# Layer 1's windowed self-attention: scores for one half's 64 keys, scores placed between projections, values last from two copies

## The chip, the cores and the metric

The kernel runs on one core of one Trainium2 chip. A time is the device time of one execution in microseconds (us). Three runs of the kernel before took 2820.73, 2821.43 and 2823.51 us; their median is 2821.43 us. The profile is of one further execution. Engines are named as in the profile: PE (TensorE matmul), PEld (TensorE weight load, which overlaps PE), DVE (VectorE), ACT (ScalarE), POOL (GpSimd) and SP (SyncE, which here issues most DMAs).

## The reference

A two-layer perceiver block works on 256 tokens of width 512 and a context of 25088 tokens, all in f32. Each layer has cross-attention, self-attention and a mixture of experts, each added to the tokens. The change concerns the self-attention of the second layer ("layer 1"), which works on windows of 128 tokens after a shift by 64:

```python
if SHIFTED:
    x = jnp.roll(x, -DISP, axis=1)              # DISP = 64, b, s, d = 1, 256, 512
xw = x.reshape(-1, w, d)                        # w = 128: two windows
qkv = xw @ w_qkv + b_qkv                        # then q, k, v of 16 heads, 32 wide
attn = jnp.einsum('nhqd,nhkd->nhqk', q, k) / jnp.sqrt(jnp.float32(d_k))
if SHIFTED:
    mask = _create_mask(w)                      # 0 between the first 64 and the last 64
    attn = jnp.where(mask == 0, jnp.float32(NEG), attn)
attn = jax.nn.softmax(attn, axis=-1)
vals = jnp.einsum('nhqk,nhkd->nhqd', attn, v)
out = vals.transpose(0, 2, 1, 3).reshape(n, w, d) @ w_o + b_o
if SHIFTED:
    out = jnp.roll(out.reshape(b, s, d), DISP, axis=1)
```

The mask sets a score to -9e15 wherever query and key lie in different halves of a window. So a token attends to the 64 keys of its own half alone, and in both windows half of the 128 x 128 scores of each head become zero weights.

## The kernel before

The 256 tokens `x` stay in SBUF as two tiles of 128 (T = 2). A normalised and transposed copy `xT` (`norm_T`, which for this layer also applies the shift while it copies) has features on the partitions, 4 blocks of 128 (DC = 4). The program is one long sequence. Most of its time goes to the context of the second cross-attention; then come the stage that is changed, a routing over 8 experts, and the experts' matmuls, whose weights are fetched by SP once the routing has produced expert numbers. The order on each engine is left to a scheduler, except that matmuls written as `queue << ...` stay in the order of the program on PE.

[...]Six form a ring (`ring`, `take`, `give`), from which `ps_mm` hands out the oldest one in turn; two more (`ps_ac`) are separate. A tile that is written into a bank has to wait until the bank's previous content has been read.

The stage in question is `self_attention`, which layer 0 uses as well. It is called from L1044 with the mask `halves` (a constant made by three POOL memsets at L146 to L148), one key block for each of the two token tiles, and `roll=64`. Its steps:

1. `norm_T` (L171): normalise, transpose on PE (L184), copy out (L187, L189).
2. `feature_major` (L198): queries for all heads, then keys, 16 matmuls each of 128x256 (L203), evicted by DVE with their bias (L209).
3. Values: for each token tile 4 matmuls of 128x512 (L239), evicted by DVE (L243).
4. `attention_blocks` (L249): for each token tile t and each group `qp` of eight heads, `weights` and then `attend` of the group before. `weights` makes eight score matmuls (L259) of 32 rows (the width of a head) by 128 keys, four heads side by side in the array's rows, and then, for each pair of heads r, adds the mask on DVE (L270), takes the maximum (L273), and exponentiates on ACT with the sum as a by-product (L275). A reciprocal (L280) and four multiplies (L282) normalise. `attend` transposes the weights on PE (L294), copies them out on any engine (L295), and multiplies with the values (L301): 128 keys deep, 32 columns wide, four heads side by side in the array's columns. DVE copies the result to `oT` while it undoes the shift (L311, L313).
5. `project_out` (L213): for each token tile four matmuls of 128x512 (L217) and two additions (L195, L196).

Weights for the stage are fetched earlier, at the end of the cross-attention, into freed buffers. The rows of biases for it come by a POOL DMA just ahead of it (L1035, L100).

Of the kernel before, what the change touches and what calls it, by code (L numbers as in the profile page):

```python
# [9 lines left out]
F32 = mybir.dt.float32  # L10
AF = mybir.ActivationFunctionType
ALU = mybir.AluOpType
AX = mybir.AxisListType
PSUM = bass.MemoryType.PSUM

P = 128
D = 512
NT = 256
T = NT // P
DC = D // P  # L20
H = 16
HD = D // H
# [5 lines left out]
SCALE = 1.0 / math.sqrt(HD)  # L28
# [9 lines left out]
def perceiver_kernel(  # L38
# [7 lines left out]
    nc = tc.nc  # L46
# [24 lines left out]
    def ps_mm(shape=None):  # L71
        tile, home = take("mm", shape)
        give(home)
        return tile
# [21 lines left out]
    rows = {}  # L96
# [45 lines left out]
        pattern=[[-1, 2 * P]], channel_multiplier=1,  # L142
    )

    halves = const.tile([P, P], F32, name="halves")
    nc.gpsimd.memset(halves, 0.0)  # L146
    nc.gpsimd.memset(halves[0:64, 64:128], -9e15)
    nc.gpsimd.memset(halves[64:128, 0:64], -9e15)  # L148


    class InOrder:

# [67 lines left out]
                )  # L220
            add_rows(t, ps, row)

    def self_attention(xT, wo, col_q, row_v, row_o, blocks, load_qkv, roll=0, fill=None):

        fill = fill or (lambda n: None)
        with tc.tile_pool(name="sa", bufs=1) as sa:
            v = sa.tile([P, T, D], F32, name="v_sa")
            oT = sa.tile([P, DC, NT], F32, name="oT")
            qT = sa.tile([P, DC, NT], F32, name="qT_sa")
            kT = sa.tile([P, DC, NT], F32, name="kT_sa")  # L230
            with tc.tile_pool(name="saw", bufs=1) as saw:
                wqkv = load_qkv(saw)
                xT = xT()
                feature_major(qT, wqkv[0], xT, col_q)
                feature_major(kT, wqkv[1], xT, col_q + 1)
                for t in range(T):
                    ps = ps_mm()
                    for dc in range(DC):
                        queue << nc.tensor.matmul(  # L239
                            ps, xT[:, dc, t * P : (t + 1) * P], wqkv[2][:, dc, :],  # L240
                            start=dc == 0, stop=dc == DC - 1,
                        )
                    nc.vector.tensor_add(v[:, t, :], ps, rows[row_v])  # L243
            with tc.tile_pool(name="sas", bufs=2) as sas:
                attention_blocks(sas, qT, kT, v, oT, blocks, roll, fill)
            fill(1)
            project_out(oT, wo, row_o)

    def attention_blocks(sas, qT, kT, v, oT, blocks, roll, fill):  # L249
        def weights(t, qp):  # L250

            keys, mask = blocks[t]
# [34 lines left out]
        def attend(t, qp, e):  # L287
            keys, _ = blocks[t]
            pT = sas.tile([P, 4, 2, 2, P], F32, tag="pT", name="pT", bufs=1)
            for r in range(4):  # L290
                tp = ps_ac([P, 2, 2, P])
                for i in range(2):
                    for kb in range(len(keys)):
                        queue << nc.tensor.transpose(tp[:, i, kb, :], e[:, r, i, kb * P : (kb + 1) * P], ident)  # L294
                nc.any.tensor_copy(pT[:, r, :, : len(keys), :], tp[:, :, : len(keys), :])  # L295
            av = ps_mm([P, 2, P])
            for i in range(2):
                for kb, kt in enumerate(keys):
                    for r in range(4):
                        h = 4 * (2 * qp + i) + r  # L300
                        queue << nc.tensor.matmul(  # L301
                            av[32 * r : 32 * r + 32, i, :],
                            v[:, kt, h * HD : (h + 1) * HD],
                            pT[:, r, i, kb, :],
                            start=kb == 0 and i == 0, stop=kb == len(keys) - 1,
                            skip_group_check=True,
                        )
            at = (t * P + roll) % NT
            first = min(P, NT - at)
            q2 = slice(2 * qp, 2 * qp + 2)  # L310
            nc.vector.tensor_copy(oT[:, q2, at : at + first], av[:, :, :first])  # L311
            if first < P:
                nc.vector.tensor_copy(oT[:, q2, : P - first], av[:, :, first:])  # L313

        pending = None
        for t in range(T):
# [5 lines left out]
                pending = (t, qp, e)  # L322
        fill(1)
        attend(*pending)

    def rank_of(pool, vals, shape):

# [485 lines left out]
    with tc.tile_pool(name="xa", bufs=2) as xa:  # L813
# [121 lines left out]
        def attend(first, last, qp, es, v):  # L935
            for i in range(2):
                for r in range(4):
                    h = 4 * (2 * qp + i) + r
                    queue << nc.tensor.matmul(  # L939
                        acc[qp][32 * r : 32 * r + 32, i, :],  # L940
                        v[:, h * HD : (h + 1) * HD], es[qp][:, 4 * i + r, :],
                        start=first and i == 0, stop=last, skip_group_check=True,
                    )
# [97 lines left out]
    nc.vector.scalar_tensor_tensor(slot, iota, float(P), ps, ALU.mult, ALU.add)  # L1041
    ffn_scope = ExitStack()
    ffn = ffn_scope.enter_context(tc.tile_pool(name="ffn", bufs=2))
    self_attention(  # L1044
        lambda: norm_T(roll=64), l1a_wo, C_L1A_BQ, R_L1A_BV, R_L1A_BO,
        [([0], halves), ([1], halves)], lambda pool: l1a_wqkv, roll=64,
    )
    ctp_scope.close()

    experts = ExitStack()  # L1050
# [292 lines left out]
```

## Time and profile before

| | |
|---|---|
| median of three runs | 2821.43 us |
| the profiled execution's own time | 2821.5 us |
| its span, first to last instruction | 2819.7 us |
| start of the stage's first projection matmul (L203) | 2465.83 us |
| last score-and-value matmul ended, output projection (L217) starts | 2518.05 us |
| last output projection result reaches DVE (L195) | 2526.56 us |
| granted TensorE clock, mean over the span | 0.985 |
| granted clock from 2488.6 to 2518 us | 0.70 |

Times inside the span are counted from its first instruction. A row of the time line has the start, the length, the engine, the source line and operation, what is written and read, the shape, the count, and in brackets how long the engine had been idle and what ended that. A row of the stretches has the busy time of each engine, with the number of instructions in brackets, then the granted clock (1.00 is full speed), the share of the DMA engines in use and GB/s. A row of the waits says who waited for whom: total, how often, longest.

In f32 a matmul leaves two records on PE and two on PEld; a transpose leaves one. "32*128" behind a matmul is the size of the stationary part: rows of the array by columns.

### The profile page before, as it was taken

What the parts mean: (1) busy time and instruction counts of PE and PEld (TensorE: products, weight loads), DVE (VectorE), ACT (ScalarE), POOL (GpSimd) and SP (SyncE); (2) the same over time, 40 slices, a digit from 0 to 9 for tenths busy, and PEclk for the clock granted to TensorE, in tenths of its full rate; (3) what the DMA queues carried; (4) which work ended last, traced back from release to release, by engine and by line L of the source; (5) the groups of instructions that cost most, each with busy time, mean ns of one, the idle gap of its engine ahead of it and who ended that gap; (6) DMA issues with size and microseconds to landing.
All of it is one profiled execution on the core that took longest, in us unless ns stands there. A gap on an engine that the chain in (4) does not pass through costs nothing. (4 is left out here: it accounts for less than half of the span.)

```text
span 2819.7 us, 57053 instructions
## 1 busy us (share of the span) xinstructions
PE 2735.0 (97%) x21390; PEld 1928.0 (68%) x21390; DVE 1733.7 (61%) x3085; ACT 1706.9 (61%) x7006; POOL 577.4 (20%) x532
## 2 busy tenths in 40 slices
PE   8998899999999999999999999999999999879998
PEld 7866777776666666666666666666666666547775
DVE  4435512267777777777777777777777777642101
ACT  6832100047778777778877878878777878631111
POOL 4321000012222222222222223232323232100000
PEclk9999999999999999999999999999999999979999
DMA  9961334421000101000100000100000101107773
GB/s 386 422 269 65 157 135 179 152 88 46 31 31 31 46 17 45 31 31 31 46 31 31 32 31 31 46 32 30 32 30 33 45 16 46 46 1 282 262 270 150
DMA packets 40548, 262.33 MB, mean 93 GB/s; under 512 B 5256, under 2 KB 8376, under 8 KB 12880
## 3 DMA queue, kind: packets, MB, share of 16 engines
q1 hardware_dynamic: 37088, 237.32, 22.2%
q0 software_dynamic: 3184, 21.33, 1.8%
q8 instruction: 174, 2.85, 0.4%
q14 instruction: 102, 0.84, 0.1%
HBM read 239.23 MB, written 19.40 MB: 92 GB/s over the span
## 5 line engine op out<-in xcount | busy, mean ns | idle before, releaser
L926 ACT ACTIVATE e<-ps_sc,nm 128x256 f32<-128x256 f32 x3136 | 1437.8, 484 | 377.3 <-DVE nm L921 376.6
L921 DVE TENSOR_REDUCE nm<-ps_sc 128x2 f32<-128x512 f32 x1568 | 994.7, 685 | 358.2 <-PE ps_sc L912 358.2
L926 ACT ACTIVATION_READ_ACCUMULATOR e<-ps_sc,nm 128x1 f32 x3136 | 678.7, 216 | 0.0
L939 PE MATMUL ps_ac<-e,vs 128*32 128x256 f32 x6272 | 420.7, 386 | 4.1 <-POOL vs L953 4.1
L428 PE MATMUL ps_kv<-ts,wq 128*128 128x256 f32 x1568 | 386.7, 390 | 5.5 <-DVE wq L392 3.7
L428 PE MATMUL ps_kv<-wq,ts 128*128 128x256 f32 x1568 | 387.1, 391 | 0.0
L953 POOL TENSOR_TENSOR vs<-v,rc 128x512 f32<-128x512 f32 x160 | 167.8, 1049 | 1016.3 <-DVE rc L947 1016.3
L428 PEld LDWEIGHTS ps_kv<-ts,wq 128*128 128x128 f32 x1568 | 285.8, 190 | 90.6 <-issue 27.3
L428 PEld LDWEIGHTS ps_kv<-wq,ts 128*128 128x128 f32 x1568 | 286.3, 190 | 84.8 <-issue 26.5
L912 PE MATMUL ps_sc<-qT,kT 32*128 32x256 f32 x4096 | 304.0, 401 | 1.5 <-ACT e L926 1.3
L939 PEld LDWEIGHTS ps_ac<-e,vs 128*32 128x32 f32 x6272 | 164.2, 109 | 202.2 <-issue 114.1
L450 DVE TENSOR_TENSOR v<-v,ps_kv 128x512 f32<-128x512 f32 x343 | 227.6, 676 | 85.1 <-PE ps_kv L428 54.8
L912 PEld LDWEIGHTS ps_sc<-qT,kT 32*128 32x128 f32 x4096 | 191.3, 184 | 116.5 <-ACT e L926 106.4
L428 PE MATMUL ps_kv<-wq,ct 128*128 128x256 f32 x1008 | 244.1, 385 | 0.0
L428 PE MATMUL ps_kv<-ct,wq 128*128 128x256 f32 x1008 | 242.4, 383 | 0.0
L450 DVE TENSOR_TENSOR kT<-kT,ps_kv 128x512 f32<-128x512 f32 x280 | 187.0, 680 | 67.6 <-PE ps_kv L428 57.5
L428 PEld LDWEIGHTS ps_kv<-wq,ct 128*128 128x128 f32 x1008 | 189.4, 191 | 38.0 <-ACT e L926 12.9
L428 PEld LDWEIGHTS ps_kv<-ct,wq 128*128 128x128 f32 x1008 | 188.1, 190 | 38.1 <-ACT e L926 12.6
L1232 ACT ACTIVATE hT<-ps_mm,b 128x128 f32<-128x128 f32 x128 | 36.6, 368 | 211.9 <-PE ps_mm L1226 158.7
L912 PE MATMUL ps_sc<-qT,kTp 32*128 32x256 f32 x2176 | 156.8, 400 | 0.0
L414 POOL TENSOR_TENSOR ts<-ct 128x512 f32<-128x512 f32 x84 | 107.1, 1275 | 230.9 <-DMA ct<-in_ctx_dram 230.8
L912 PEld LDWEIGHTS ps_sc<-qT,kTp 32*128 32x128 f32 x2176 | 99.5, 184 | 58.7 <-ACT e L926 55.2
(252 smaller groups left out, 2220.2 us busy)
## 6 DMA issues: line engine op xcount, KB each, us to landing
ct<-in_ctx_dram SPq DMA_DIRECT2D x67, 1024.0 KB, 5.0
we<-in_l1e_dram SPq DMA_DIRECT2D x64, 1024.0 KB, 6.9
we<-in_l0e_dram SPq DMA_DIRECT2D x17, 1536.0 KB, 8.1
cs<-in_ctx_dram SPq DMA_DIRECT2D x17, 1024.0 KB, 14.7
we0o<-in_l0e_dram SPq DMA_DIRECT2D x17, 768.0 KB, 4.4
kv<-kT POOLq DMA_DIRECT2D x9, 1024.0 KB, 9.5
kv<-v POOLq DMA_DIRECT2D x9, 1024.0 KB, 9.4
vp<-kv SPq DMA_DIRECT2D x9, 1024.0 KB, 4.7
```

Of the source, the lines that this page charges most:

```text
L414: queue << nc.gpsimd.tensor_sub(ts[:, k], a, b)
L428: queue << nc.tensor.matmul(ps[:, m, :], fixed[:, d, m * P : (m + 1) * P], moving[:, d, :], start=d == 0, stop=d == 1,)
L450: queue << nc.vector.tensor_tensor(to, old, ps, ALU.subtract if a == W_A22 else ALU.add)
L912: queue << nc.tensor.matmul(sc[r][:, i, :], kTs[c][part, 2 * qp + i, s * P : (s + 1) * P], qT[part, 2 * qp + i, :], start=True, stop=True,)
L921: queue << nc.vector.tensor_reduce(nm[:, 2 * qp : 2 * qp + 2, r], sc[r], AX.X, ALU.max, negate=True)
L926: queue << nc.scalar.activation(e[:, 4 * i + r, :], sc[r][:, i, :], AF.Exp, bias=nm[:, q, r : r + 1], accum_out=sm[:, q, r : r + 1],)
L939: queue << nc.tensor.matmul(acc[qp][32 * r : 32 * r + 32, i, :], v[:, h * HD : (h + 1) * HD], es[qp][:, 4 * i + r, :], start=first and i = ...
L953: queue << nc.gpsimd.tensor_mul(vs.rearrange("p (h d) -> p h d", h=H), vs_of[c, s].rearrange("p (h d) -> p h d", h=H), rc.unsqueeze(2).to_ ...
L1232: nc.scalar.activation(hT[:, fc, :], ps[:, fc, :], AF.Gelu, bias=b1[:, hf * FC + fc : hf * FC + fc + 1])
```

## The change

Layer 1's attention gets a function of its own, `window_attention`. `self_attention` stays for layer 0 and loses the parameter `roll`; the constant `halves` goes.

- Queries and keys are projected by blocks of 128 features (`queries_and_keys(fc)`: four heads). The queries are scaled when they are evicted. Keys of the first two blocks are evicted by ACT, the others by DVE.
- `weights(qp)` makes the scores of eight heads for both token tiles at once. A matmul takes the 64 queries and 64 keys of one half (`b`) of a window, of one head; its result lands on that half's 64 partitions of a PSUM tile. No mask is added. The maximum is read straight from PSUM, then come 16 exponentials of 128x64 in four groups, each with its own reciprocal and multiply.
- The order on PE: projections of blocks 0 and 1, scores of the first eight heads, projections of blocks 2 and 3, scores of the other eight heads, the value projection, the transposes of both groups, the values of both groups, the output projection.
- `transposed(e)` turns 128 columns at once, which are two heads (i = 0 and 1) of 64 keys each. So the weights of head i lie on partitions 64i to 64i+63, whichever half b of the window they belong to. The matmul in `attend` needs weights and values on the same partitions. Where b = i the values `v` are in place; for the others `v_swapped` holds a copy of `v` with the 64-partition halves exchanged, made by four DMAs of 128 KB on SP's queue.
- `attend` has 64 keys in the rows, 32 columns, and 64 queries as the moving part. DVE and ACT copy the results to `oT`, shifted back by 64.

```diff
@@ -141,11 +141,6 @@
         out=band, in_=band, compare_op=ALU.is_ge, fill=-1e30, base=P,
         pattern=[[-1, 2 * P]], channel_multiplier=1,
     )
-    halves = const.tile([P, P], F32, name="halves")
-    nc.gpsimd.memset(halves, 0.0)
-    nc.gpsimd.memset(halves[0:64, 64:128], -9e15)
-    nc.gpsimd.memset(halves[64:128, 0:64], -9e15)
     class InOrder:
@@ -220,9 +215,8 @@
                 )
             add_rows(t, ps, row)
-    def self_attention(xT, wo, col_q, row_v, row_o, blocks, load_qkv, roll=0, fill=None):
-        fill = fill or (lambda n: None)
+    def self_attention(xT, wo, col_q, row_v, row_o, blocks, load_qkv, fill):
         with tc.tile_pool(name="sa", bufs=1) as sa:
             v = sa.tile([P, T, D], F32, name="v_sa")
             oT = sa.tile([P, DC, NT], F32, name="oT")
@@ -242,11 +236,11 @@
                         )
                     nc.vector.tensor_add(v[:, t, :], ps, rows[row_v])
             with tc.tile_pool(name="sas", bufs=2) as sas:
-                attention_blocks(sas, qT, kT, v, oT, blocks, roll, fill)
+                attention_blocks(sas, qT, kT, v, oT, blocks, fill)
             fill(1)
             project_out(oT, wo, row_o)
-    def attention_blocks(sas, qT, kT, v, oT, blocks, roll, fill):
+    def attention_blocks(sas, qT, kT, v, oT, blocks, fill):
         def weights(t, qp):
             keys, mask = blocks[t]
@@ -305,12 +299,7 @@
                             start=kb == 0 and i == 0, stop=kb == len(keys) - 1,
                             skip_group_check=True,
                         )
-            at = (t * P + roll) % NT
-            first = min(P, NT - at)
-            q2 = slice(2 * qp, 2 * qp + 2)
-            nc.vector.tensor_copy(oT[:, q2, at : at + first], av[:, :, :first])
-            if first < P:
-                nc.vector.tensor_copy(oT[:, q2, : P - first], av[:, :, first:])
+            nc.vector.tensor_copy(oT[:, 2 * qp : 2 * qp + 2, t * P : (t + 1) * P], av)
         pending = None
         for t in range(T):
@@ -322,6 +311,126 @@
                 pending = (t, qp, e)
         fill(1)
         attend(*pending)
+    def window_attention(xT, wqkv, wo, col_q, row_v, row_o):
+        wq, wk, wv = wqkv
+        HT = P // 2
+        with tc.tile_pool(name="wa", bufs=1) as wa, tc.tile_pool(name="was", bufs=2) as was:
+            v, v_swapped = (wa.tile([P, T, D], F32, name=n) for n in ("v_wa", "v_swapped"))
+            qT, kT, oT = (wa.tile([P, DC, NT], F32, name=n) for n in ("qT_wa", "kT_wa", "oT_wa"))
+            def queries_and_keys(fc):
+                for res, w, col in ((qT, wq, col_q), (kT, wk, col_q + 1)):
+                    ps = ps_mm([P, NT])
+                    for dc in range(DC):
+                        queue << nc.tensor.matmul(
+                            ps, w[:, dc, fc * P : (fc + 1) * P], xT[:, dc, :],
+                            start=dc == 0, stop=dc == DC - 1,
+                        )
+                    b = cols[:, col, fc : fc + 1]
+                    if res is qT:
+                        nc.vector.tensor_scalar(res[:, fc, :], ps, b, SCALE, ALU.add, ALU.mult)
+                    elif fc > 1:
+                        nc.vector.tensor_scalar(res[:, fc, :], ps, b, None, ALU.add)
+                    else:
+                        nc.scalar.activation(res[:, fc, :], ps, AF.Identity, bias=b)
+            def weights(qp):
+                sc = [ps_mm([P, T, 2, HT]) for _ in range(4)]
+                for t in range(T):
+                    for i in range(2):
+                        for b in range(2):
+                            half = slice(t * P + b * HT, t * P + (b + 1) * HT)
+                            for r in range(4):
+                                part = slice(32 * r, 32 * r + 32)
+                                queue << nc.tensor.matmul(
+                                    sc[r][b * HT : (b + 1) * HT, t, i, :],
+                                    qT[part, 2 * qp + i, half], kT[part, 2 * qp + i, half],
+                                    start=True, stop=True, skip_group_check=True,
+                                )
+                e = was.tile([P, 4, 2 * T, HT], F32, tag="e_wa", name="e_wa")
+                nm, sm, rc = (was.tile([P, 4, 2 * T], F32, tag=n, name=n) for n in ("nm_wa", "sm_wa", "rc_wa"))
+                for r in range(4):
+                    s = sc[r].rearrange("p t i j -> p (t i) j")
+                    nc.vector.tensor_reduce(nm[:, r, :], s, AX.X, ALU.max, negate=True)
+                    for k in range(2 * T):
+                        nc.scalar.activation(
+                            e[:, r, k, :], s[:, k, :], AF.Exp, bias=nm[:, r, k : k + 1],
+                            accum_out=sm[:, r, k : k + 1],
+                        )
+                    nc.vector.reciprocal(rc[:, r, :], sm[:, r, :])
+                    nc.vector.tensor_mul(
+                        e[:, r], e[:, r], rc[:, r].unsqueeze(2).to_broadcast([P, 2 * T, HT])
+                    )
+                return e
+            def transposed(e):
+                pT = was.tile([P, 4, T, P], F32, tag="pT_wa", name="pT_wa")
+                for k in range(2):
+                    tp = ps_mm([P, 2, T, P])
+                    for r in range(2):
+                        for t in range(T):
+                            queue << nc.tensor.transpose(
+                                tp[:, r, t, :],
+                                e[:, 2 * k + r, 2 * t : 2 * t + 2, :].rearrange("p i j -> p (i j)"), ident,
+                            )
+                    if k == 0:
+                        nc.vector.tensor_copy(pT[:, 0:2], tp)
+                    else:
+                        nc.scalar.copy(pT[:, 2:4], tp)
+                return pT
+            def attend(qp, pT):
+                av = [ps_mm([P, T, P]) for _ in range(2)]
+                for values, swap in ((v, 0), (v_swapped, 1)):
+                    for t in range(T):
+                        for r in range(4):
+                            for i in range(2):
+                                b = i ^ swap
+                                h = 4 * (2 * qp + i) + r
+                                queue << nc.tensor.matmul(
+                                    av[i][32 * r : 32 * r + 32, t, b * HT : (b + 1) * HT],
+                                    values[i * HT : (i + 1) * HT, t, h * HD : (h + 1) * HD],
+                                    pT[i * HT : (i + 1) * HT, r, t, b * HT : (b + 1) * HT],
+                                    start=True, stop=True, skip_group_check=True,
+                                )
+                for i in range(2):
+                    a = av[i].rearrange("p t j -> p (t j)")
+                    copy = nc.vector.tensor_copy if i == 0 else nc.scalar.copy
+                    copy(oT[:, 2 * qp + i, HT:], a[:, : NT - HT])
+                    copy(oT[:, 2 * qp + i, :HT], a[:, NT - HT :])
+            queries_and_keys(0)
+            queries_and_keys(1)
+            e0 = weights(0)
+            queries_and_keys(2)
+            queries_and_keys(3)
+            e1 = weights(1)
+            for t in range(T):
+                ps = ps_mm()
+                for dc in range(DC):
+                    queue << nc.tensor.matmul(
+                        ps, xT[:, dc, t * P : (t + 1) * P], wv[:, dc, :],
+                        start=dc == 0, stop=dc == DC - 1,
+                    )
+                nc.vector.tensor_add(v[:, t, :], ps, rows[row_v])
+                for b in range(2):
+                    nc.sync.dma_start(
+                        out=v_swapped[b * HT : (b + 1) * HT, t, :],
+                        in_=v[(1 - b) * HT : (2 - b) * HT, t, :],
+                    )
+            pT0 = transposed(e0)
+            pT1 = transposed(e1)
+            attend(0, pT0)
+            attend(1, pT1)
+            project_out(oT, wo, row_o)
     def rank_of(pool, vals, shape):
@@ -1041,10 +1150,7 @@
     nc.vector.scalar_tensor_tensor(slot, iota, float(P), ps, ALU.mult, ALU.add)
     ffn_scope = ExitStack()
     ffn = ffn_scope.enter_context(tc.tile_pool(name="ffn", bufs=2))
-    self_attention(
-        lambda: norm_T(roll=64), l1a_wo, C_L1A_BQ, R_L1A_BV, R_L1A_BO,
-        [([0], halves), ([1], halves)], lambda pool: l1a_wqkv, roll=64,
-    )
+    window_attention(norm_T(roll=64), l1a_wqkv, l1a_wo, C_L1A_BQ, R_L1A_BV, R_L1A_BO)
     ctp_scope.close()
     experts = ExitStack()
```

## The prediction

> **What bounds the kernel now.** I read the engine totals first, then the time line of layer 1's attention, then the waits there, then the granted clock. Every line below is of the profiled execution: span 2819.7 us, its own time 2821.5 us (1.8 us lie around the span); the median of the runs is 2821.43 us.
>
> ```profile
> PE 2735.0 (97%) x21390; PEld 1928.0 (68%) x21390; DVE 1733.7 (61%) x3085; ACT 1706.9 (61%) x7006; POOL 577.4 (20%) x532
> ```
>
> Over the whole span PE is the bound. The changed stage is two short pieces of it, and there it is different. From the time line:
>
> ```profile
> 2465.83 15.91 PE L203 MATMUL ps_mm<-xT,wct 128*128 128x256 f32 x64 [0.78 <-DVE xT L187]
> 2481.57 7.03 PE L239 MATMUL ps_mm<-wct,xT 128*128 128x512 f32 x16
> 2488.53 2.26 PE L259 MATMUL ps_mm<-kT_sa,qT_sa 32*128 32x128 f32 x32
> 2490.43 1.28 ACT L275 ACT_TABLE_LOAD   x1 [27.33 <-DVE nm_sa L273]
> 2496.21 2.24 PE L294 MATMUL ps_ac<-ident,e_sa 128*128 128x128 f32 x8 [5.42 <-DVE e_sa L282]
> 2498.39 1.59 PE L301 MATMUL ps_mm<-pT,v_sa 128*32 128x128 f32 x16
> 2503.88 0.36 PEld L301 LDWEIGHTS ps_mm<-pT,v_sa 128*32 128x32 f32 x10 [0.20 <-DVE pT L295]
> 2518.05 8.46 PE L217 MATMUL ps_mm<-wts,oT 128*128 128x512 f32 x16
> 2526.56 0.69 DVE L195 TENSOR_TENSOR tmp<-ps_mm,rows 128x512 f32<-128x512 f32 x1 [1.07 <-PE ps_mm L217]
> ```
>
> The third column is how long the group ran; "x64" are 64 records for 32 matmuls, since each f32 matmul leaves two. Projections run dense until 2488.5. From there to 2518.05 is the softmax and attention: 29.5 us in which PE was busy 17.7 (second line below). The output projection then ends at 2526.5: 60.7 us from the first L203. The waits of this stretch say who keeps PE idle:
>
> ```profile
> PE ps_ac L294 <- DVE e_sa L282: 11.4, 4, 5.4
> ```
>
> And the busy time by stretches (PE, PEld, DVE, ACT, POOL, then the granted clock, the DMA share and GB/s):
>
> ```profile
> 2488.60:2518.00 29.40, 17.71 (x161) 11.12 (x160) 20.88 (x60) 20.26 (x79) 0.00 (x0) 0.70 0.00 1
> 2489.00:2490.00 1.00, 1.00 (x18) 0.81 (x10) 1.00 (x4) 0.00 (x0) 0.00 (x0) 1.00 0.00 0
> ...
> 2516.00:2517.00 1.00, 1.00 (x9) 0.49 (x8) 0.00 (x0) 0.73 (x2) 0.00 (x0) 0.50 0.00 0
> 2518.00:2519.00 1.00, 1.00 (x2) 0.50 (x2) 0.49 (x2) 0.31 (x1) 0.00 (x0) 0.50 0.00 0
> ```
>
> Four times (11.4 us) the transposes wait for the normalised weights: DVE's mask pass, maximum, ACT's exponentials, reciprocal and multiply form a serial chain, with nothing left for PE. The granted clock says the rest: the idle PE falls to half speed, and even the first output projection matmuls (L217, 2518 on) run at 0.50. So this stage is bound by the softmax chain plus a cold PE, not by matmul work.
>
> **The change part by part.** Only the stage from 2465.83 on is rewritten; the instruction order of everything before it is the same, and what follows depends on its last addition.
>
> *Start.* Three POOL memsets (0.20, 0.14, 0.15 us) for the mask go. POOL idles 3.49 us behind them for the first context transfer: worth nothing.
>
> *Projections.* The same 40 matmuls. The first four run cold now (L203 starts 2465.83, its first result reaches DVE at 2469.65) and will again: 3.6 us. The other 28 cost 0.432 each (DVE takes a result every 1.73 us for four): 12.1. Values: 8 x 0.86 = 6.9 (7.03 for 8). Sum 22.6, on the path, as now.
>
> *Scores.* 64 matmuls (128 records) of 32 rows x 64 columns in place of 32 matmuls (64 records) of 32x128. This shape is not in the trace. Below: weight loads followed each other at 0.036 (L301, ten in 0.36). Above: 0.071 (L259, 32 records in 2.26). Nearest is L259 within its group: 18 records started in the microsecond from 2489 at full clock, 0.055. I take 0.055: 128 x 0.055 = 7.0 us (4.6 to 9.1). A rule speaks against this part: the Trainium skill, "TensorEngine Tiling (Array Packing)", Instruction Overhead, says that a matmul with one column costs as much as one with 60, and that no tiling factor should be taken from a dimension that is already small; "TensorE: Matmul & The Clock Gate" (Wait — 56ns, not 53.3ns?) puts the issue of a matmul at about 62 ns where the hardware does not decode. By 0.062 scores and values together would cost 15.9 instead of 14.1, or 1.8 us more. The row has 0.055, below that figure, so I go by the row; both agree that halving the columns buys PE nothing, and twice the instructions do cost.
>
> *Softmax.* Per call of the new weights function: 4 maxima straight from PSUM (L273: 0.41 each), 16 exponentials of 128x64, 4 reciprocals (0.2), 4 multiplies (0.42). The mask pass (16 x 0.41 on DVE) is gone, the scale rides on the query's eviction. An exponential followed another after 0.39 us at 128 columns, and the instruction itself is 0.096 shorter from 256 to 128; so 0.34 at 64, 16 in 5.4 us (6.2 at 0.39). First call: scores run 2474.5 to 2478.0, ACT from about 2478.8 to 2484.2, behind 16 projection matmuls of 6.9 us (2478.0 to 2484.9). Its last two score banks are the first two of the second call, needed at 2484.9: 0.7 us to spare. Second call: scores end 2488.4, ACT from 2489.2 to 2494.6, multiply to 2495.4, behind the value projection (to 2495.3); its transposes come second, at 2496.4: 1 us to spare. So the chain is hidden; uncovered it costs its 7 us twice. The exponential's table load (1.28, now on the path as shown) falls behind the first scores. ACT also takes two key evictions (about 0.48 each) ahead of the first scores; the eight matmuls of head group 0 cover the last. For small waits I add 0.4 us in all.
>
> *Transposes.* 16 instead of 32, warm ones 0.13 apart (0.54 for four weight loads): 2.1 us, after the values. Copies out (128x512, 0.69 on DVE, about 0.6 on ACT) trail by one group; the second ends before its values are wanted.
>
> *The swapped copy.* Four transfers of 128 KB on SP's queue, SBUF to SBUF, waiting for the value evictions. Not in the trace; a 256 KB store took 2.0 us, a 16 KB load on POOL's queue 4.5 and a 1 MB load 4.9. The last starts at about 2496.8, lands 2498.8 (2501.7 at the worst), and is wanted by the swapped matmuls of the second token tile at about 2500: hidden, worst 1.7 us. I take 2.0, the nearest in kind. Queued behind them on SP is only the reading of the expert numbers (first weight transfer now at 2543.04), which needs the whole stage anyhow. Nothing on POOL is passed.
>
> *Values last.* 64 matmuls (128 records) of 64x32 by 64 columns for 32 (64 records) of 128x32 by 128. Again not in the trace: below 0.036, above 0.099 (L301 cold, 16 in 1.59); the warm ten records from 2503.88 to 2504.44 give 0.056. I take 0.055: 7.0 us (4.6 to 12.7).
>
> *Output projection.* 8 x 0.86 = 6.9, warm, against 8.46 now, since PE has no gap ahead of it.
>
> *Sum.* 22.6 + 7.0 + 0.4 + 2.1 + 7.0 + 6.9 = 46.0 us against 60.7: 14.7 less. Everything behind shifts with the last addition (experts' weights are requested only after routing). The clock was granted again 3.2 us after the first expert matmul (2548.24 to 2551.5); with steps of 3.41 us between its changes (2493.5, 2500.3, 2507.1), a stage shifted by 14.7 meets them about 0.9 us later, at half speed 0.4. Net 14.3: 2821.4 - 14.3 = 2807.
>
> **The rivals.**
> - *Packing is partly lost or cold.* The records cost 0.09, halfway between L301's warm row (0.076, 16 in 1.21) and its cold row (0.099): 256 x 0.09 = 23.0 for 14.1, and 2816. For: the cold row is this very operation after transposes (2516 above). Against: PE has no gap here, and scores follow projections.
> - *A chain is late.* The second softmax at 0.5 us per exponential (8 us), or a slow copy, stops PE for 1.5 to 3 us: 2809.5. For: margins of about 1 us. Against: no ACT row is that slow at 64 columns.
> - *Slower: small tiles do not overlap at all.* Each record pays its weight load (0.109, L301) and then its stream (the 0.86 of a 128x512 matmul are two records of 0.43, so 0.054 for 64 columns): 0.16 x 256 = 41.5, 27.4 more than in my sum, 13 us slower: 2834. It decides from 0.11 us per record on ((14.1 + 14.3) / 256). For: the last value burst of the layer before took 3.36 us for 32 records, 0.105 at 256 columns. Against: that had four times the columns, and L259 and L301 stay at 0.055 to 0.076 warm.
> That the change does not do what it says is no rival: the instruction order on each engine has the new shapes and transfers.
>
> **How the numbers follow.** My case 0.64 (2802 to 2812: records at 0.036 give 2802, at 0.066 plus small waits 2812), late chain 0.13, lost packing 0.15, no overlap 0.08. 0.2% is 5.6 us, about what a measurement of this kernel can tell from no change: 2815.8 and below is faster. The lost packing case straddles that, a third of it falls within. Faster 0.64 + 0.13 + 0.10 = 0.87, same 0.05, slower 0.08. The range takes my case, the late chain and half of the lost packing: 2802 to 2815.
>
> **What would show it.** Right: from the first projection to the end of the output projection about 46 us; scores in two bursts of 3.5 us; no idle PE over 1 us between; a granted clock of 1.00 from the fifth projection matmul to the end of the output projection; the table load under the first scores; the four copies landed before PE asks. Wrong: bursts over 5 us, a wait of the transposes for the second softmax, the swapped matmuls waiting for a transfer, or a clock of 0.5 in the values.

## The result and the profile after

The changed kernel takes 2799.19 us (median; 2797.43 to 2799.3) against 2822.22 before, measured side by side: a ratio of 0.9917, with 0.99 to 0.9934 as its 95% interval. It is faster by 23.0 us, where 14.3 were predicted, and it lies below the predicted range of 2802 to 2815. The profiled execution of after has a span of 2797.6 us and a time of its own of 2799.3.

PE is still the bound over the whole span: it is busy for 2721.9 us, 97% as before. The time line of the stage after the change, in the same columns:

```profile
2467.90 8.97 PE L330 MATMUL ps_mm<-xT,wct 128*128 128x256 f32 x32 [0.78 <-DVE xT L182]
2476.80 0.37 PE L351 MATMUL ps_mm<-kT_wa,qT_wa 32*64 32x64 f32 x16
...
2477.40 1.28 ACT L362 ACT_TABLE_LOAD   x1
2477.43 0.78 PE L351 MATMUL ps_mm<-kT_wa,qT_wa 32*64 32x64 f32 x48 [0.26 <-ACT kT_wa L340]
2478.14 7.17 PE L330 MATMUL ps_mm<-xT,wct 128*128 128x256 f32 x32
...
2485.25 0.37 PE L351 MATMUL ps_mm<-kT_wa,qT_wa 32*64 32x64 f32 x16
2485.90 0.78 PE L351 MATMUL ps_mm<-kT_wa,qT_wa 32*64 32x64 f32 x48 [0.28 <-DVE kT_wa L338]
2486.61 7.13 PE L419 MATMUL ps_mm<-wct,xT 128*128 128x512 f32 x16
...
2493.58 1.91 PE L379 MATMUL ps_mm<-ident,e_wa 128*128 128x128 f32 x16
2495.42 0.45 PE L398 MATMUL ps_mm<-pT_wa,v_wa 64*32 64x64 f32 x32
2495.68 0.46 PE L398 MATMUL ps_mm<-pT_wa,v_swapped 64*32 64x64 f32 x16
2496.74 0.30 PE L398 MATMUL ps_mm<-pT_wa,v_swapped 64*32 64x64 f32 x2 [0.60 <-DMA v_swapped<-v_wa]
2497.36 0.28 PE L398 MATMUL ps_mm<-pT_wa,v_swapped 64*32 64x64 f32 x7 [0.32 <-DMA v_swapped<-v_wa]
...
2498.37 7.10 PE L212 MATMUL ps_mm<-wts,oT_wa 128*128 128x512 f32 x16
...
2505.51 0.69 DVE L190 TENSOR_TENSOR tmp<-ps_mm,rows 128x512 f32<-128x512 f32 x1 [1.07 <-PE ps_mm L212]
```

From the first projection matmul to the moment when DVE reads the last result of the output projection, the stage takes 2505.51 - 2467.90 = 37.61 us; before it was 60.73. The projections run on without a break around two bursts of scores (2476.80 to 2478.14, 2485.25 to 2486.61), and the output projection follows the values at once. The starts give the length of each piece:

| piece | predicted us | measured us |
|---|---|---|
| projections of queries and keys | 15.7 | 8.90 + 7.11 = 16.0 |
| projection of values | 6.9 | 6.97 |
| scores, two bursts | 7.0 | 1.34 + 1.36 = 2.70 |
| transposes | 2.1 | 1.84 |
| values | 7.0 | 2.95 |
| output projection | 6.9 | 7.14 |
| small waits | 0.4 | in the pieces |
| sum | 46.0 | 37.6 |

Scores and values were put at 14.0 us and took 5.65, of which 1.46 are waits (0.26 + 0.28 for keys, 0.60 + 0.32 for copies). These 8.35 us are the miss of 8.4 us in the stage; the other pieces are each within 0.4 us and nearly cancel.

The busy time in stretches of after shows the other part of the gain, the clock:

```profile
2467.90:2506.20 38.30, 36.10 (x368) 24.29 (x368) 16.71 (x44) 15.55 (x75) 0.00 (x0) 0.95 0.06 15
2478.00:2485.00 7.00, 7.00 (x46) 6.07 (x39) 4.71 (x15) 5.53 (x33) 0.00 (x0) 1.00 0.00 0
2498.00:2499.00 1.00, 1.00 (x40) 0.65 (x29) 0.75 (x4) 0.79 (x5) 0.00 (x0) 1.00 0.06 16
```

PE is busy for 36.1 of 38.3 us. The first output projection matmuls run at 1.00, where they had 0.50 before, and the second row holds ACT's exponentials (5.53 us) under a PE that is never idle.

From stage to span: 23.12 us less in the stage, a start that is 2.07 us later, and 1.05 us less behind the stage, together 22.1 = 2819.7 - 2797.6. The predicted 14.3 fell short of this by 7.8: 8.4 in the stage and 1.45 behind it (0.4 lost was predicted), less the 2.07 of the start. The later start isn't the change's: it is taken up with the run of the memsets below. The 1.05 come from the phase of the clock. The expert matmuls of before, and those of after:

```profile
2548.27 5.34 PE L1226 MATMUL ps_mm<-xg,we 128*128 128x128 f32 x32 [1.23 <-DVE g L1139]
```

```profile
2527.29 3.81 PE L1332 MATMUL ps_mm<-xg,we 128*128 128x128 f32 x32 [1.18 <-DVE g L1245]
```

The same 32 records took 1.53 us less, more than the whole 1.05, since the granted clock had come back by 2526.2 in after, ahead of them, and only at 2551.5 in before, 3.2 us into them. The runs below bear this out: where these records took 3.81 us, the stretch from the stage to the end took 291.8 to 292.2 us, and where they took 5.4 to 5.9, it took 294.0 to 294.4 (one exception: the run with wide scores, 3.81 and 294.9).

### The profile page after: what moved, and what is told of

Read it like the earlier page. It is cut to its first block, busy times and chain, and to the rows that moved or that the text cites. A ratio compares the mean times of both kernels' runs of the same rounds, so it can differ in the third digit from the quotient of the medians.

```text
span 2797.6 us, 57238 instructions
## 1 busy us (share of the span) xinstructions
PE 2721.9 (97%) x21502; PEld 1920.9 (69%) x21502; DVE 1721.7 (62%) x3052; ACT 1700.9 (61%) x7001; POOL 577.5 (21%) x529
## 3 DMA queue, kind: packets, MB, share of 16 engines
q1 hardware_dynamic: 37408, 237.85, 22.6%
```

## The experiments

Two theories of the cheap small matmuls stood against each other at first. *Tiles in use*: a small matmul occupies its tile of TensorE's array for about 0.21 us (an estimate: the old score matmuls took 0.11 us with four tiles in turn, so each held its tile for some 0.43, and the new ones have half the columns), and the more different tiles take turns (eight in the scores of after), the less each costs: 0.21 / 8 = 0.027. *Backlog*: a small matmul always cost as little, and before it only looked dear, since PE waited there for its inputs one by one, while now the instructions stand ready behind a dense projection. In every run below "stage" is measured as above.

**Fewer tiles in turn.** Scores one row group after the other, so that two tiles take turns, not eight; values one row half after the other:

```diff
-                for t in range(T):
-                    for i in range(2):
-                        for b in range(2):
...
-                            for r in range(4):
+                for r, t, i, b in ((r, t, i, b) for r in range(4) for t in range(T) for i in range(2) for b in range(2)):
...
-                    for t in range(T):
-                        for r in range(4):
-                            for i in range(2):
+                for swap, i, t, r in ((s, i, t, r) for s in range(2) for i in range(2) for t in range(T) for r in range(4)):
```

> Same matmuls as the changed kernel, other order: scores take one head row r after another (the two halves b alternate, so only two of the eight 32x64 tiles are in use at a time), values take one row half i after the other (four of the eight 64x32 tiles). Theory 'tiles in use': a tile is busy for its weight load and its stream, twice per f32 matmul[...], and the time per matmul is that over the number of tiles in use. Scores 0.107 us per matmul, 3.4 us per burst of 32 in place of 0.9; values about 0.04 per matmul. Stage about 5 us longer. Rival 'backlog': matmuls were slow before only because PE's queue ran dry; then the order does not matter, 0.027 per matmul, bursts as in the changed kernel.

The first score burst on the time line of this kernel, from its wait for the key eviction to the projection behind it:

```profile
2476.42 1.45 PE L348 MATMUL ps_mm<-kT_wa,qT_wa 32*64 32x64 f32 x60 [0.30 <-ACT kT_wa L340]
2477.80 7.17 PE L330 MATMUL ps_mm<-xT,wct 128*128 128x256 f32 x32
```

60 records are 30 matmuls, in 2477.80 - 2476.42 = 1.38 us: 0.046 each. In after it is 24 in 0.71 (2477.43 to 2478.14), 0.030. So these two tiles, which share their rows of the array, are somewhat dearer, but not the 0.107 of tiles in use. The values behind the last copy took 0.93 us for 36 matmuls, 0.026. The kernel took 2801.45 us in one run, its stage 38.88.

**The other order.** Scores of one column half after the other (four tiles in turn), values one column group after the other:

```diff
+                for b, t, i, r in ((b, t, i, r) for b in range(2) for t in range(T) for i in range(2) for r in range(4)):
...
+                for swap, r, t, i in ((s, r, t, i) for s in range(2) for r in range(4) for t in range(T) for i in range(2)):
```

> Same matmuls again: scores take all matmuls of one column half b and then of the other (four tiles in use), values take one column group r after another (two tiles in use). 'Tiles in use': scores 0.053 us per matmul, bursts of 1.7 us; values about 0.08 per matmul, 32 of a group in 2.6 us. 'Backlog': as in the changed kernel, 0.027 and 0.9 us.

The same two lines of this kernel's time line:

```profile
2474.24 0.95 PE L348 MATMUL ps_mm<-kT_wa,qT_wa 32*64 32x64 f32 x56 [0.29 <-ACT kT_wa L340]
2475.12 7.17 PE L330 MATMUL ps_mm<-xT,wct 128*128 128x256 f32 x32
```

28 matmuls in 0.88 us: 0.031, and the values 0.028 (45 in 1.28), though they had only two tiles in turn, in different rows. That is about the price of after. Tiles in use, in its simple form, falls: 0.053 and 0.08 were asked for. Time 2796.66 us in one run, stage 38.32.

**Wide scores in the new place.** 16 matmuls of 32x128 by 128 per burst, as in the kernel before, where after has 32 of 32x64 by 64:

```diff
-                        for b in range(2):
-                            half = slice(t * P + b * HT, t * P + (b + 1) * HT)
...
-                                    sc[r][b * HT : (b + 1) * HT, t, i, :],
-                                    qT[part, 2 * qp + i, half], kT[part, 2 * qp + i, half],
+                                sc[r][:, t, i, :],
+                                qT[part, 2 * qp + i, t * P : (t + 1) * P],
+                                kT[part, 2 * qp + i, t * P : (t + 1) * P],
```

> The changed kernel, but its scores made as before by 16 matmuls per burst of 32x128 tiles and 128 keys, in the new places. It leaves out that the second half of the tokens reads its own keys: the softmax takes the first 64 keys for all tokens. 'Tiles in use': four tiles of 0.43 us per matmul, 0.107 per matmul, 1.7 us per burst, so 0.8 us longer than 32 small ones although half as many instructions. 'Backlog': 16 x 0.027 = 0.45 us, shorter than the small ones, up to the 0.85 us that the stream itself needs at 128 columns.

Its time line, the first score burst on PE and its weight loads (PEld):

```profile
2476.19 1.58 PE L349 MATMUL ps_mm<-kT_wa,qT_wa 32*128 32x128 f32 x32
2476.83 0.76 PEld L349 LDWEIGHTS ps_mm<-kT_wa,qT_wa 32*128 32x128 f32 x24 [0.32 <-ACT kT_wa L340]
2477.71 7.17 PE L330 MATMUL ps_mm<-xT,wct 128*128 128x256 f32 x32
```

16 matmuls in 1.52 us look like 0.095 each, and the expectations of the next two runs use that figure. But this burst, too, waits for the key eviction after its first four matmuls. PE's row shows no gap, since the records ahead of it count as running through most of the wait; the row of the weight loads does show it. From 2476.83 on, 12 matmuls took 0.88 us: 0.073 each. The run with the order alone, below, has the same 12 in 0.88 (2486.10 to 2486.98). So backlog's 0.85 us for the whole burst falls (16 at 0.073 are 1.17), and so does tiles in use with 0.107. But the 0.11 that the prediction read from L259 wasn't the price of that shape either. Two stretches of L259 in the profile before (number, ns shortest/median/longest, first and last start):

```profile
L259 PE MATMUL ps_mm<-kT_sa,qT_sa x16: 270/270/372, 2488.5 to 2489.0; 32*128 32x128 f32 x16
L259 PE MATMUL ps_mm<-kT_sa,qT_sa x16: 270/270/372, 2489.1 to 2490.5; 32*128 32x128 f32 x16
```

The first eight matmuls of the row started dense, in about 0.55 us: 0.069 each. The other eight were spread over 1.4 us. What these waited for the trace doesn't name; DVE was still reading PSUM then (L243 to 2489.33, L270 to 2490.04), which would fit a wait for banks; no run tried it. For the scores, then, backlog holds a part of the way (0.11 to about 0.07), and the smaller tile the rest (to 0.030).

The total (2804.62 us in one run) isn't comparable: here one copy was late, PE waited 1.67 us for it, and the clock was 0.50 from 2498.4 to 2501.6, where the output projection begins.

**Which width counts.** The two mixed shapes: first weights of 64 queries against 128 keys, then weights of 128 queries against 64 keys.

```diff
-                                    qT[part, 2 * qp + i, half], kT[part, 2 * qp + i, half],
+                                    qT[part, 2 * qp + i, half], kT[part, 2 * qp + i, t * P : (t + 1) * P],
...
```

> The changed kernel, but each score matmul takes 64 queries as before and all 128 keys of the window as its moving part (32 matmuls of 32x64 tiles, 128 columns); the softmax takes the first 64 keys for all tokens, the others are left unread. It tells apart what made 32x128 by 128 cost 0.095 us and 32x64 by 64 only 0.027. If the weight load (queries, 128 or 64 columns) sets it: still about 0.027 to 0.03 per matmul, burst below 1.0 us. If the streamed columns (keys) set it: about 0.05 per matmul, 1.7 us.

Time line of this kernel, from the wait on:

```profile
2476.19 0.99 PE L351 MATMUL ps_mm<-kT_wa,qT_wa 32*64 32x128 f32 x48 [0.16 <-ACT kT_wa L340]
2477.11 7.17 PE L330 MATMUL ps_mm<-xT,wct 128*128 128x256 f32 x32
```

```diff
+                                sc[r][:, t, i, :HT],
+                                qT[part, 2 * qp + i, t * P : (t + 1) * P],
+                                kT[part, 2 * qp + i, t * P : t * P + HT],
...
```

> The changed kernel with 16 score matmuls per burst of 32x128 tiles (128 queries as weights) and 64 keys as the moving part; all queries of a window meet its first 64 keys, so the second half's own keys are left out. It closes the square: 32x128 by 128 cost 0.095 us, 32x64 by 128 0.038, 32x64 by 64 0.030 per matmul. If the width of the weights sets the price: 0.08 to 0.095, burst of 1.3 to 1.5 us. If the streamed columns do: 0.05, burst of 0.8 us.

And of the other one:

```profile
2476.43 0.90 PE L349 MATMUL ps_mm<-kT_wa,qT_wa 32*128 32x64 f32 x24 [0.18 <-ACT kT_wa L340]
2477.26 7.17 PE L330 MATMUL ps_mm<-xT,wct 128*128 128x256 f32 x32
```

24 matmuls in 0.92 us and 12 in 0.83. Price per score matmul, all four from the wait for keys to the start of the next projection:

| us per matmul | 128 moving columns | 64 moving columns |
|---|---|---|
| weights 32x128 | 0.073 | 0.069 |
| weights 32x64 | 0.038 | 0.030 |

Halving the weights' columns takes the price to about half (0.073 to 0.038, 0.069 to 0.030). Halving the moving columns takes off 6% with the wide weights (0.88 to 0.83 us) and 23% with the narrow ones (0.92 to 0.71). Neither forecast was met exactly: 0.038 lies between 0.03 and 0.05, and 0.069 between 0.05 and 0.08. Narrow weights also have eight tiles taking turns where wide ones have four, but that isn't what makes them cheap: in the other order four tiles of 32x64 cost 0.031.

The two kernels took 2798.45 and 2805.11 us, one run each; the second is again one with a late copy (2.19 us of waiting, and an output projection of 9.56 us).

**One half of the change at a time.** First the 64 keys and the swapped copy in the old order (all projections, then scores and softmax, then values):

```diff
-            queries_and_keys(0)
-            queries_and_keys(1)
-            e0 = weights(0)
-            queries_and_keys(2)
-            queries_and_keys(3)
-            e1 = weights(1)
+            for fc in range(DC):
+                queries_and_keys(fc)
...
-            pT0 = transposed(e0)
-            pT1 = transposed(e1)
-            attend(0, pT0)
-            attend(1, pT1)
+            e0 = weights(0)
+            e1 = weights(1)
+            attend(0, transposed(e0))
+            attend(1, transposed(e1))
```

> The half scores, the swapped copy and all small tiles kept, the order put back: all projections and the values first, then both score bursts, then transposes, values. Theory 'both parts': the softmax of both groups is uncovered. From the changed kernel's rows: projections and values 22.6 us, scores 0.9, first maximum 0.7, 32 exponentials 0.29 apart 9.4, last reciprocal and multiply 0.6, transposes, copy and values of the second group 2.6, a cold output projection 8.4, waits 0.5: 45.7 us from the first projection to the end of the output projection in place of 37.6, so the end 8 us later than the changed kernel, about 15 us earlier than the kernel before. Rival 'the half scores are all of it': within 2 us of the changed kernel.

It took 2807.75 us (0.9946, 0.9929 to 0.9962), its stage 45.81. The chain of the softmax is open again; PE's waits in the stage, and then a stretch of it with PE's busy time, the granted clock, the DMA share and GB/s:

```profile
PE ps_mm L398 <- ACT pT_wa L386: 2.7, 2, 2.4
PE ps_mm L351 <- ACT e_wa L362: 2.4, 2, 1.5
...
2493.00:2502.90 9.90, 6.43 (x88) 0.50 0.00 0
```

The stage came out as expected (45.7), but partly by luck: the clock was back at 2503, and the output projection took 7.17 us where a cold one of 8.4 was expected (2503.63 to 2510.80), so what is ahead of it took 1.3 us longer than reckoned.

Then the new order with all 128 keys and the mask, without swapped copies:

```diff
+                    nc.vector.tensor_tensor(
+                        s, sc[r], halves.unsqueeze(1).to_broadcast([P, 2 * T, P]), ALU.add
+                    )
+                    nc.vector.tensor_reduce(nm[:, r, :], s, AX.X, ALU.max, negate=True)
...
+                                av[i][32 * r : 32 * r + 32, t, :],
+                                v[:, t, h * HD : (h + 1) * HD], pT[:, r, 2 * t + i, :],
...
```

> The new order kept, the half scores undone: 128 keys with the mask added on DVE, exponentials of 128x128, 32 transposes, values from 128 keys, no swapped copy. Theory 'both parts': per group DVE has 4 x (0.69 mask + 0.69 maximum + 0.69 multiply) and evictions, 10 to 11 us against the 6.9 us that the projections cover, so PE waits 3 to 4 us for each group; values take 32 matmuls of about 0.15 (4.9 us) in place of 1.7, transposes 3.8 in place of 1.9: 46 us (43 to 49) for the stage, 8 us later than the changed kernel, 14 us earlier than the kernel before. Rival 'the order is all of it': within 2 us of the changed kernel. Rival 'the half scores are all of it': within 3 us of the kernel before.

It took 2804.63 us (0.9933, 0.9917 to 0.995), its stage 42.13, less than the 43 to 49 expected. Its time line from the second scores on:

```profile
2486.10 0.95 PE L353 MATMUL ps_mm<-kT_wa,qT_wa 32*128 32x128 f32 x24 [1.85 <-DVE kT_wa L343]
2486.98 8.83 PE L416 MATMUL ps_mm<-wct,xT 128*128 128x512 f32 x16
...
2499.23 1.95 PE L396 MATMUL ps_mm<-pT_wa,v_wa 128*32 128x128 f32 x64
2501.11 7.13 PE L217 MATMUL ps_mm<-wts,oT_wa 128*128 128x512 f32 x16
```

and the clock in a stretch of it:

```profile
2487.10:2490.40 3.30, 3.30 (x4) 0.50 0.00 0
```

The last key eviction stands on DVE behind mask, maxima and multiplies of the first softmax: PE waits 1.85 us for it, and the projection of values behind it starts at a clock of 0.50 and takes 8.83 us in place of 7.13. What I had misjudged is the row of L396: the old shape of the values, 128x32 by 128, takes 1.88 us for 32 matmuls, 0.059 each, where I had reckoned with 0.15 and the row of the kernel before had given 0.112. So part of that row was waiting, not the price of the tile: for the values, backlog holds more than half of the way (0.112 to 0.059), and the smaller tile does the rest (0.059 to 0.026).

The order alone takes 18.6 us from the stage, the halves alone 14.9, both together 23.1: they overlap, since the order hides the softmax that the halves shorten.

**Are the memsets the later start?** The three memsets of the mask put back, with nobody reading them:

```diff
+    halves = const.tile([P, P], F32, name="halves")
+    nc.gpsimd.memset(halves, 0.0)
+    nc.gpsimd.memset(halves[0:64, 64:128], -9e15)
+    nc.gpsimd.memset(halves[64:128, 0:64], -9e15)
```

> The changed kernel with the mask constant's three POOL memsets put back at the start. The changed kernel reached layer 1's attention 2.07 us later than the kernel before (2467.90 against 2465.83 us), although nothing before it was meant to change. If the missing memsets did it (POOL's rows transfer starts 0.5 us earlier and meets the first weight and context transfers), the stage starts near 2465.8 again and the end comes 2 us earlier. If it is scatter of the first transfers between executions, the start lies anywhere between 2464 and 2469 and does not follow the memsets.

The first matmul of the stage, with the memsets back:

```profile
2469.01 9.05 PE L335 MATMUL ps_mm<-xT,wct 128*128 128x256 f32 x32 [0.78 <-DVE xT L187]
```

It starts later still. Time 2800.2 us (one run), stage 37.69.

**The changed kernel once more**, without an edit:

> The changed kernel once more, beside the others on one chip: about 23 us below the kernel before, a stage of 37.6 us. The start of the stage should again lie anywhere between 2464 and 2469 us if that is scatter.

Its first matmul of the stage on the time line:

```profile
2469.14 9.05 PE L330 MATMUL ps_mm<-xT,wct 128*128 128x256 f32 x32 [0.78 <-DVE xT L182]
```

2798.2 us (0.9909, 0.9893 to 0.9926), stage 37.69, and a start at 2469.14 where the first profile had 2467.90. Over all profiles with a rewritten stage the start lies between 2464.63 and 2469.14, whatever was changed, and the 2465.83 of before lies among them: scatter of the work ahead of the stage. The stage itself repeats within 0.1 us.

**The waits for the copies.** PE waited 0.60 + 0.32 us for swapped values. Half of the copies issued on ACT's queue, and the values of both head groups that need no copy done first:

```diff
-                    nc.sync.dma_start(
+                    (nc.sync, nc.scalar)[b].dma_start(
...
-            attend(0, pT0)
-            attend(1, pT1)
+            attend(pT0, pT1)
...
```

> The changed kernel with one of each two swapped copies issued by ACT in place of SP, and PE taking the values of both groups from v before any from the copy. In the changed kernel PE waited 0.60 and 0.32 us for the copies. If the copy is what the values wait for, these waits go, and the stage is 0.9 us shorter; by the time alone that cannot be told from the changed kernel (0.03%). If ACT's issue delays its softmax or its copies, the transposes or values start later and nothing is gained.

The end of its values and its output projection:

```profile
2495.06 0.45 PE L397 MATMUL ps_mm<-pT_wa,v_swapped 64*32 64x64 f32 x30 [0.22 <-DMA v_swapped<-v_wa]
2496.06 7.10 PE L212 MATMUL ps_mm<-wts,oT_wa 128*128 128x512 f32 x16 [0.56 <-PE ps_mm L397]
```

The wait for copies shrank to 0.22 us, but now the results of both head groups come together at the end, and the output projection waits 0.56 us for them. The gain is given back: 2797.33 us (0.9908, 0.9892 to 0.9925), stage 37.66. The queues alone, with the order of after:

```diff
-                    nc.sync.dma_start(
+                    (nc.sync, nc.scalar)[b].dma_start(
```

> The changed kernel with the second of each two swapped copies issued by ACT, and the values in their old order. The run with both edits ended its stage after 37.7 us as the changed kernel does (37.6): the wait for the copies went, and 0.56 us came back as a wait of the output projection for the first group's late results. With the old order that should not come back: stage 36.9 us, 0.7 shorter. Rival: ACT's issue comes in between its exponentials, the second softmax ends later and the transposes wait: 37.6 or more.

2798.59 us (0.991, 0.9894 to 0.9927), stage 37.70 where 36.9 was expected. From issue to landing the copies of after took 2.2 to 2.4 us (median 2.3), those of this kernel 2.4 to 2.9 (median 2.7). What they gain by an earlier issue they lose in flight, and PE waits 0.57 + 0.22 us. Neither version is measurably faster than the changed kernel.

## Why the prediction was wrong

- **Start.** Three memsets at nothing: right, and the start's 2 us are scatter.
- **Projections.** 22.6 us predicted, 16.0 + 6.97 measured. Right, with the first four cold: the granted clock was 0.50 until 2471.6.
- **Scores: this is the step that failed, together with the values.** "I take 0.055: 128 x 0.055 = 7.0 us (4.6 to 9.1)." The rest of the argument held, the hidden softmax and the warm clock above all; this price was wrong, and in two ways. First the reading: the "x18" of the microsecond from 2489 counts the records that were running in it; twelve of them had started before it and only six in it. Dense, the old shape took 0.034 to 0.037 per record (0.069 per matmul at the head of L259, 0.073 in the wide runs). Then the carrying over: the price was used unscaled for a tile half as wide, since "halving the columns buys PE nothing, and twice the instructions do cost". The square of four prices shows the opposite: half the weights' columns, about half the price. Together the matmul went from 0.110 over about 0.07 to 0.030, so 0.015 per record, and the bursts took 2.70 us with two waits of 0.26 and 0.28 in them. The lower bound of 0.036 was no bound either: it is about what the old, wider tile costs dense.
- **Values.** The same price of 0.055, 7.0 us against 2.95 with 0.92 of waiting in it; 0.026 per matmul. Here L301's ten warm records held waiting, as the dense 0.059 per matmul of the old shape shows against 0.112; the smaller tile did the rest. There the weights keep their 32 columns, while rows and moving columns were halved together; no run separates these two.
- **The rule weighed against the row.** The Trainium skill, "TensorEngine Tiling (Array Packing)", Instruction Overhead, advises against taking a tiling factor from a dimension that is already small; its equal cost goes up to 60 columns, so it doesn't say, as the prediction has it, that a step from 128 to 64 buys nothing. Behind the wait for keys, three quarters of a burst took 0.88 us in 12 wide matmuls and 0.71 in 24 small ones: the split saved a fifth. The 62 ns of issue that I set beside the row were not seen in any run. Nor does the other figure of that page hold here, "TensorE: Matmul & The Clock Gate" (Wait — 56ns, not 53.3ns?), by which starts come no closer than about 25 ns: the first 16 value matmuls of after, 32 records, started within 0.26 us (2495.42 to 2495.68), 0.016 per matmul and 0.008 per record. The measurement decides.
- **Softmax.** Hidden, as predicted. ACT's exponentials repeat every 0.29 us (2478.70, 2479.00, 2479.29 on the time line; 0.34 predicted), and the first softmax ends on ACT at 2483.5, with projections to 2485.25. The table load lies at 2477.40 to 2478.68, under scores and projection.
- **Transposes and copies.** 1.84 us for 2.1. The copies took 2.2 to 2.4 us for 2.0. They weren't fully hidden: the last was issued at 2495.0 and asked for at 2497.04 (2497.36 less its wait of 0.32), 2.0 us later, where the prediction had 3.2 (2496.8 to 2500); with the third copy's 0.60 PE waited 0.92. That follows from the same failed term, since the values ahead of it went by so fast.
- **Output projection.** 7.14 for 6.9, warm: right.
- **Behind the stage.** 0.4 us were to be lost to the clock's phase, 1.05 were gained. The prediction took the times at which the clock changes as fixed against the span, but they aren't: 2526.2 and 2551.5 lie 25.3 us apart, 7.4 of the steps of 3.41. So the sign of this term was chance. (Its sum was also a little off: 14.7 less four steps of 3.41 leaves 1.06, not 0.9.)
- **Rivals.** Packing lost, a late chain and small tiles without overlap all ended on the wrong side: all three make records dearer or PE idle. The case that came true, a record far cheaper than any that the prediction took from the trace, had no place in the range.

Still open: why two tiles that share their rows cost 0.046 in the scores, while two in different rows (values, 0.028) and four or eight cost 0.026 to 0.031. The runs give the price, not what the hardware overlaps within a tile. In the two runs with weights of 128 queries one copy took 3.7 and 4.2 us in place of 2.3; whether that is chance or comes of the edit wasn't tried.

## What to carry to other kernels

A price per matmul read from a row belongs to that row's shape: in the scores here it followed the weights' columns first and the moving columns second. Before taking a row as a price or as a lower bound, look whether it holds waits: take the first and last start of its dense part, look at the weight loads too, and don't take the number of records that overlap a stretch for the number that started in it. Putting independent projections between scores and values paid twice here, since it hid the softmax and kept the clock at 1.00 for the work behind it (with the old order it was 0.50 from 2493.0 to 2502.9). When one piece shrinks far more than reckoned, look at once for the transfer that was hidden by its old length.

## What the runs showed of the hardware

- Small f32 matmuls (32x64 by 64, 64x32 by 64) took 0.026 to 0.031 us each in nearly every order of tiles; the exception was 0.046, for scores with two tiles in turn that share their rows.
- In the scores the weights' columns set that price more than the moving columns do: 0.073, 0.069, 0.038 and 0.030 for 128 by 128, 128 by 64, 64 by 128 and 64 by 64 (weights' columns by moving columns, 32 rows). The Trainium skill, "TensorE: Matmul & The Clock Gate" (LDWEIGHTS), has the load of weights take a time in proportion to their columns and not to their rows; the square fits the part on columns. No run here varies the rows alone or separates load from stream.
- Copies within SBUF of 128 KB landed 2.2 to 2.4 us after issue from one queue (once 3.7 and once 4.2) and 2.4 to 2.9 with two queues at once.
- PE's waits of up to 0.6 us left the granted clock at 1.00 (after); a wait of 1.85 us was followed by 3.4 us at 0.50, although PE was busy again (the order alone, 2487.0 to 2490.4).
